# Fewer changes between full-width and column-tiled products in a two-layer attention kernel

## The chip, the cores and the metric

The kernel runs on one core of a Trainium2 chip. The metric is device time in microseconds for one execution over the whole input. Before the change the median of three runs is 2829.34 us (2828.06 to 2830.42), and the profiled execution spans 2826.2 us.

## The reference

The input `x` has 8 images of 256 channels and 96 x 96 points. Two residual layers follow each other, each behind a group norm `gn` (32 groups, no scale or shift). All arithmetic is in float32.

```
# layer 0
z   = gn(x)
q,k,v = fft2(w1 z + b1), fft2(w2 z + b2), fft2(w3 z + b3)      # 256 channels each
q,k = q/|q|, k/|k|                                             # norm over the 9216 points
a   = einsum('bhcn,bhdn->bhcd', q, k) * temperature            # 8 heads of 32 channels, no conjugate
a   = softmax(real(a)) + 1j * softmax(imag(a))
x   = x + w_out abs(ifft2(a v))
# layer 1
z   = gn(x)
q,k = softplus(Wq z + bq), softplus(Wk z + bk)                 # 32 channels each
v   = Wv z + bv                                                # 256 channels
x   = x + q (k v^T) / (q . (sum(k) + 1e-6))                    # linear attention
```

## The kernel before

The program handles one image after another (b = 0 to 7). Two large SBUF tiles, the arenas, hold an image each: the one being worked on, and in turn the rotated image `y` or the next `x`.

**No Fourier transform is carried out.** By Parseval's rule the logits and the norms of layer 0 follow from two 256 x 256 matrices: the Gram matrix of x with itself (for the norms) and the one of x with x read backwards in both directions (for the logits). `pair_sums(b)` forms the sum and the difference of each point with its mirror point (`eo`, on DVE or GpSimd, L305/L306), transposes them on TensorE (`eoT`, L338), evacuates them on ScalarE (L341) and adds their products into two PSUM accumulators (`products`, L319). Their sum and their difference are the two matrices, `cov[0]` and `cov[1]`. Both are symmetric, so only the blocks 00, 01 and 11 of 128 x 128 are accumulated.

**`attention(b)`** (L358) makes the small matrices of layer 0. It gets mean and deviation by group (`group_norm`, L258); lays the channel means on one partition (`mu`, L368); forms the constant terms of q and k (`qkm`, L379/L384); subtracts 2 HW mu mu^T from the accumulator by a product of one row (L395), which centres the sums; closes the accumulation with the last `products` (L397); forms `cov` (L403 to L406); transposes block 01 of both matrices to get block 10 (`covT`, L410); scales the rows by the deviation (L413); multiplies with the weights (`cw`, L424, for the norms, from four blocks; L435 for the logits); and then the softmax. The result is `mz`, which takes y to the channels of the attention output.

**`rotate(b)`** (L525) writes `y`, each row of the image times a constant matrix of its own, in steps of two rows: four transposes (`xr`, L547), evacuation on ScalarE (L558), four products with those matrices, `tm` (L550) and evacuation on DVE (L554). The `tm` tiles hold TR = 4 rows, in a pool of four buffers (L531), loaded through ScalarE's queue. The rows 0 to 3, 48 to 51 and 92 to 95 come last.

**`images(b)`** (L580) goes through 24 chunks of 384 points. `z` (L619) applies `mz` to `y`: real and imaginary parts of 16 channels of each head as full-width products (two of 128 columns), and channel 16 of the eight heads as one of 32 columns. For this `z16`, four chunks are computed at once on the four 32-column tiles of TensorE, every fourth chunk (L638 to L648); the tile `v16` has two buffers. Then come the modulus (ScalarE L660/L662/L663 and GpSimd L661), the output projection `po` (L631), the residual addition (L633) and the statistics for layer 1.

**`layer1(b)`** (L674) scales its weights by the deviation (`wkq` L683; `wvs` L724, from a resident copy `wv`), forms k and q on column tiles (`kq`, L711), and then goes through 18 steps of 128 points in four strands. A step transposes x (`xT`, L770, 8 transposes into two PSUM tiles), evacuates one tile on DVE (L775) and one on ScalarE (L773), and adds k x of the step before into `kx` (L748: four products on the four column tiles, each in two passes). k itself is transposed in six pieces (`kT`, L761), and softplus is finished along the way on DVE and ScalarE (L737 to L741). The loop around L748 is

```
if pend is not None:
    add_kx(*pend)
pend = (i, xt, kq(0, s)[...])
```

**`output(b)`** (L821) multiplies q by the reciprocal denominators (select on TensorE L826, product on DVE L828), forms `o` (L841), adds it to x on DVE and, through ScalarE, on GpSimd (L846 to L850), and stores.

**Order of the work.** `weave` advances one generator by what the other yields: the steps of `rotate(b)` fill `attention(b)`, and the steps of `pair_sums(b + 1)` fill the end of `images`, `layer1` and `output`. The last image has no following sums. A planner orders the instructions of each engine from priorities; where `manual_schedule` is named (PE in `attention`, and PE, DVE, GpSimd and SyncE in `output`) the order is that of the program. PSUM has five `ps` tiles and three `acc` tiles.

Of the kernel before, what the change touches and what calls it, by code (L numbers as in the profile page):

```python
# [47 lines left out]
F32 = mybir.dt.float32  # L49
AF = mybir.ActivationFunctionType  # L50
ALU = mybir.AluOpType
# [3 lines left out]
KC = 2  # L55
# [3 lines left out]
TR = 4  # L59
# [8 lines left out]
def two_layer_kernel(ctx: ExitStack, tc: tile.TileContext, x, w1t, b1, w2t, b2, w3, b3, wot, temp,  # L68
# [11 lines left out]
    assert C == KC * P and H == W and TW == 2 * CH and NT == 2 * NS and NC == 2 * NT and W <= P and PR == TR  # L80
# [4 lines left out]
    four = ctx.enter_context(tc.tile_pool(name="four", bufs=4))  # L85
# [39 lines left out]
    def ps_tile(name):  # L125
        return psum.tile([P, 512], F32, tag="ps", name=name)
# [60 lines left out]
    nc.vector.memset(half[0:W], 0.5 ** 0.5)  # L187
    epsb = const.tile([P, 1], F32, name="epsb")
# [4 lines left out]
    wv = const.tile([P, KC, C], F32, name="wv")  # L193
    nc.scalar.dma_start(out=wv, in_=wvt.rearrange("(k p) o -> p k o", p=P))
# [163 lines left out]
    def attention(b):  # L358
# [5 lines left out]
        w12, w3n = wl[:, :, 0:2 * C], wl[:, :, 2 * C:3 * C]  # L364
        nmean, rstd, mv, dm = yield from group_norm(st0, f"a{b}")
        pm = ps_tile(f"mu_{b}")
        for k in range(KC):
            nc.tensor.matmul(pm[0:1, k * P:(k + 1) * P], lhsT=mv[:, k, 0:1], rhs=ident, start=True, stop=True)  # L368
        scr = [ring_tile(f"scr{i}_{b}") for i in range(3)]
        mu = scr[0][0:1, 4 * C:6 * C].rearrange("p (c n) -> p c n", c=2)  # L370
        nc.vector.tensor_copy(mu[:, 0, :], pm[0:1, 0:C])
        nc.vector.tensor_scalar_mul(mu[:, 1, :], mu[:, 0, :], -2.0 * HW)
        nc.vector.tensor_mul(dm, dm, rstd)
# [3 lines left out]
        for k in range(KC):  # L377
            for m in range(KC):
                nc.tensor.matmul(pb[32 * m:32 * m + 1, 0:2 * P], lhsT=dm[:, k:k + 1],  # L379
                                 rhs=w12[:, k, :].rearrange("p (c n) -> p c n", c=2)[:, :, m * P:(m + 1) * P],  # L380
                                 start=(k == 0), stop=False, skip_group_check=True)
# [6 lines left out]
        qkm = [scr[1][32 * m:32 * m + 1, 0:6 * P].rearrange("p (i c n) -> p i c n", i=3, c=2) for m in range(KC)]  # L388
        for m in range(KC):
            nc.scalar.copy(qkm[m][:, 0], pb[32 * m:32 * m + 1, 0:2 * P].rearrange("p (c n) -> p c n", c=2))  # L390
            nc.vector.tensor_scalar_mul(qkm[m][:, 1], qkm[m][:, 0], 2.0 * HW)
            nc.vector.tensor_mul(qkm[m][:, 2], qkm[m][:, 0], qkm[m][:, 1])

        for m in range(KC):
            nc.tensor.matmul(acc[0][:, m * C:m * C + (KC - m) * P], lhsT=mu[:, 1, m * P:(m + 1) * P],  # L395
                             rhs=mu[:, 0, m * P:C], start=False, stop=False, skip_group_check=True)
        products(*pending, False, True)  # L397
        yield 1


        CW = 3 * P
        odd = scr[2][:, 4 * C:4 * C + CW]
        nc.scalar.copy(odd, acc[1][:, 0:CW])  # L403
        cov = scr[2][:, 0:4 * C].rearrange("p (c n) -> p c n", c=2)
        nc.vector.tensor_add(cov[:, 0, 0:CW], acc[0][:, 0:CW], odd)
        nc.vector.tensor_sub(cov[:, 1, 0:CW], acc[0][:, 0:CW], odd)  # L406
        yield 2
        pt = ps_tile(f"covT_{b}")
        for c in range(2):
            nc.tensor.transpose(pt[:, c * P:(c + 1) * P], cov[:, c, P:2 * P], ident)  # L410
        nc.scalar.copy(cov[:, :, CW:CW + P], pt[:, 0:2 * P].rearrange("p (c n) -> p c n", c=2))
        for k in range(KC):
            nc.vector.tensor_scalar_mul(cov[:, :, k * C:(k + 1) * C], cov[:, :, k * C:(k + 1) * C], rstd[:, k:k + 1])  # L413
# [7 lines left out]
        for m in range(KC):  # L421
            pv = ps_tile(f"cw_{b}_{m}")
            for k in range(KC):
                nc.tensor.matmul(pv, lhsT=block(0, k, m), rhs=w12[:, k, :], start=(k == 0), stop=(k == KC - 1))  # L424
# [3 lines left out]
            r = slice(32 * m, 32 * m + 1)  # L428
# [96 lines left out]
    def rotate(b):  # L525
# [4 lines left out]
        def load_r(h):  # L530
            tm = four.tile([W, TR, W + 1], F32, tag="tm", name=f"tm_{b}_{h}")  # L531
# [29 lines left out]
        last = (0, H // 2, H - TR)  # L561
        groups = [*(g for g in range(0, H, TR) if g not in last), *last]
        tms = [load_r(g) for g in groups[0:2]]
        pending = []
        for h in [g + i for g in groups for i in range(0, TR, 2)]:
            if h % TR == 0:
                i = groups.index(h)
                tm = tms.pop(0)
                if i + 2 < len(groups):
                    tms.append(load_r(groups[i + 2]))  # L570
# [9 lines left out]
    def images(b):  # L580
# [56 lines left out]
        for i in range(NC):  # L637
            if i % 4 == 0:  # L638
                p16 = ps_tile(f"z16_{b}_{i}")
                for k in range(KC):  # L640
                    for j, r in enumerate(blocks(2)):
                        apply(p16[r], k, 2, j, i + j)
                v16 = two.tile([P, CH], F32, tag="v16", name=f"v16_{b}_{i}")
                v3 = v16.rearrange("p (q h) -> p q h", h=H)
                nc.vector.tensor_add(v3, p16[:, 0:CH].rearrange("p (q h) -> p q h", h=H),
                                     tab16.unsqueeze(1).to_broadcast([P, PR, H]))
                nc.scalar.activation(v16, v16, AF.Square)
                nc.gpsimd.tensor_add(v3, v3, sg[2].unsqueeze(1).to_broadcast([P, PR, H]))  # L648
# [12 lines left out]
            nc.gpsimd.tensor_add(e[:, 0:2, :], e[:, 0:2, :], e[:, 2:4, :])  # L661
            nc.scalar.activation(e[:, 0:2, :], e[:, 0:2, :], AF.Sqrt)  # L662
            nc.scalar.activation(e[0:NH, 1, :], v16[32 * (i % 4):32 * (i % 4) + NH, :], AF.Sqrt)  # L663
            pending.append((i, e))
            if len(pending) > 2:
                project(*pending.pop(0))
# [7 lines left out]
    def layer1(b):  # L674
# [47 lines left out]
        for k in range(KC):  # L722
            nc.vector.tensor_scalar_mul(nmb[:, k, :], ones, nmean[:, k:k + 1])
            nc.vector.tensor_scalar_mul(wvs[:, k, :], wv[:, k, :], rstd[:, k:k + 1])  # L724
# [26 lines left out]
        pend = None  # L751
        softplus(0, 0)
        for s in range(NS):
# [9 lines left out]
            for i in range(s * CH // P, (s + 1) * CH // P):  # L763
                xt = [xt_slot(), xt_slot()]
# [17 lines left out]
        add_kx(*pend)  # L782
# [38 lines left out]
    def output(b, x, kq, rec, am):  # L821

        def normalize(s):
            t, g = divmod(s, 4)
            pd = ps_tile(f"rec_{b}_{s}")
            nc.tensor.matmul(pd[:, 0:CH], lhsT=sel8[32 * g:32 * g + 32, t * P:(t + 1) * P], rhs=rec[32 * g:32 * g + 32],  # L826
                             start=True, stop=True)
            nc.vector.tensor_mul(kq(1, s), kq(1, s), pd[:, 0:CH])  # L828

        for s in range(4):  # L830
            normalize(s)
        yield 1
        for s in range(4, NS):
            normalize(s)
        for s in range(NS):
            for m in range(KC):
# [6 lines left out]
                for j in range(NB):  # L843
# [91 lines left out]
```

## Time and profile before

| | |
|---|---|
| median of three runs | 2829.34 us |
| profiled span | 2826.2 us |
| TensorE (PE) busy | 2776.0 us |
| VectorE (DVE) busy | 2001.3 us |
| ScalarE (ACT) busy | 1358.4 us |
| GpSimd (POOL) busy | 871.0 us |
| one image, from one images stage to the next | 347.8 us |
| kx (L748) | 1152 records, 96.5 us |
| z and z16 (L619) | 2400 records, 600.9 us |
| cw for the norms (L424) | 64 records, 30.5 us |
| mu (L368), the one-row product (L395) | 4.8 us and 7.3 us |

A float32 product appears as two records (two passes), a transpose as one. A record such as `128*32 128x257` names the stationary tile (128 rows, 32 columns) and the moving tile. The busy time of PE counts the union of pipelined records, so that what one group costs is read better from the distance between its start and the next one's. "Idle before, releaser" is the time for which an engine waited, and for whom.

### The profile page before, as it was taken

How to read it: one execution, taken by the hardware profiler on the slowest of the kernel's cores; microseconds unless marked ns; L12 is line 12 of the kernel's file. 1: busy time of each engine (PE TensorE's matmuls, PEld its weight loads, DVE VectorE, ACT ScalarE, POOL GpSimd, SP SyncE). 2: the span in 40 equal slices, each digit the busy share in tenths (PEclk: the TensorE clock that was granted, in tenths of full speed). 3: DMA queues.
4: the chain of work that ended last, by engine and by line, in shares of the span. 5: the costliest groups of instructions: out<-in, count | busy, mean ns of one | idle time of the engine just before them, and what ended most of it. 6: DMA issues, size and time to landing. Idle time of an engine off the chain costs nothing.

```text
span 2826.2 us, 48343 instructions
## 1 busy us (share of the span) xinstructions
PE 2776.0 (98%) x18548; PEld 1984.4 (70%) x18548; DVE 2001.3 (71%) x4103; ACT 1358.4 (48%) x2066; POOL 871.0 (31%) x976
## 2 busy tenths in 40 slices
PE   8999999999999999999999999999999999999988
PEld 8965679656795667956688566785668856688556
DVE  7587765877658776587675876758766687666767
ACT  3455534555345553455533545345554455434553
POOL 4033430343303424035140351413514135231311
PEclk9999999999999999999999999999999999999997
DMA  5120151201412015120152201521015210151003
GB/s 168 37 72 11 33 183 42 72 5 48 168 47 72 3 46 172 47 68 2 46 175 51 62 3 46 177 59 52 3 46 179 63 45 3 57 171 28 1 3 135
DMA packets 196933, 190.72 MB, mean 67 GB/s; under 512 B 90272, under 2 KB 196704, under 8 KB 196704
## 3 DMA queue, kind: packets, MB, share of 16 engines
q1 hardware_dynamic: 128288, 162.25, 18.0%
q10 hardware_dynamic: 68416, 25.38, 3.8%
q8 instruction: 148, 2.42, 0.4%
q14 instruction: 81, 0.66, 0.1%
HBM read 112.01 MB, written 75.57 MB: 66 GB/s over the span
## 4 chain that ended last, share of the span: by engine, by line
PE 94%; DVE 2%; ACT 2%; issue 1%; DMA 0%; POOL 0%; POOLq 0%; ACTq 0%
PE z L619 20%; PE po L631 17%; PE acc L319 13%; PE y L550 11%; PE xr L547 6%; PE eoT L338 5%; PE kq L711 5%; PE xT L770 3%; PE o L841 3%; PE kx L748 3%; PE cw L424 1%; DVE arena L741 1%; ACT spu L739 1%; PE mz L511 1%; PE kT L761 1%
## 5 line engine op out<-in xcount | busy, mean ns | idle before, releaser
L619 PE MATMUL z<-arena,mz 128*128 128x384 f32 (+4 forms) x2400 | 600.9, 478 | 0.0
L631 PE MATMUL po<-e,wo 128*128 128x384 f32 x1536 | 529.8, 487 | 0.2 <-ACT e L662 0.2
L661 POOL TENSOR_TENSOR e<-e 128x768 f32<-128x768 f32 x192 | 348.4, 1816 | 511.6 <-ACT e L660 511.6
L619 PEld LDWEIGHTS z<-arena,mz 128*128 128x128 f32 (+1 forms) x2400 | 321.0, 163 | 254.1 <-issue 61.9
L550 PE MATMUL y<-tm,xT 96*128 96x97 f32 x3072 | 477.5, 261 | 1.7 <-POOL tm L533 1.5
L550 PEld LDWEIGHTS y<-tm,xT 96*128 96x128 f32 x3072 | 463.3, 192 | 13.1 <-issue 8.4
L319 PE MATMUL acc<-xT 128*128 128x256 f32 (+2 forms) x2368 | 442.8, 328 | 0.0
L656 DVE TENSOR_TENSOR e<-z,xT 128x768 f32<-128x768 f32 x384 | 366.2, 954 | 101.7 <-PE z L619 98.9
L631 PEld LDWEIGHTS po<-e,wo 128*128 128x128 f32 x1536 | 289.9, 190 | 197.3 <-DVE arena L633 1.2
L253 DVE BATCH_NORM_STATS2 st<-arena 128x6 f32<-128x384 f32 x768 | 406.4, 553 | 14.2 <-DMA arena<-in_x_dram 2.6
L547 PE MATMUL xr<-ident,arena 128*96 128x128 f32 x1536 | 414.2, 276 | 0.0
L319 PEld LDWEIGHTS acc<-xT 128*128 128x128 f32 (+1 forms) x2368 | 381.3, 191 | 36.1 <-issue 2.9
L558 ACT COPY xT<-xr 96x512 f32<-96x512 f32 x384 | 221.8, 582 | 303.7 <-PE xr L547 288.5
L554 DVE COPY arena<-y 128x384 f32<-128x384 f32 x384 | 213.6, 556 | 203.4 <-PE y L550 201.5
L305 POOL TENSOR_TENSOR eo<-arena 128x760 f32<-128x760 f32 x150 | 273.4, 1823 | 256.6 <-issue 133.5
L660 ACT ACTIVATE e<-e 128x1536 f32<-128x1536 f32 x192 | 284.6, 1482 | 101.2 <-DVE e L656 100.8
L662 ACT ACTIVATE e<-e 128x768 f32<-128x768 f32 x192 | 161.9, 843 | 334.3 <-POOL e L661 333.5
L633 DVE TENSOR_TENSOR arena<-arena,po 128x384 f32<-128x384 f32 x384 | 211.6, 553 | 95.7 <-PE po L631 71.9
L341 ACT ACTIVATE xT<-eoT 128x512 f32<-128x512 f32 x280 | 167.0, 597 | 194.9 <-PE eoT L338 192.9
L533 POOL COPY tm<-csn 96x4 f32<-96x4 f32 x192 | 38.1, 199 | 647.1 <-PE y L550 610.6
L547 PEld LDWEIGHTS xr<-ident,arena 128*96 128x96 f32 x1536 | 229.4, 150 | 10.9 <-issue 7.4
L850 POOL TENSOR_TENSOR arena<-arena,po 128x384 f32<-128x384 f32 x96 | 95.4, 1004 | 364.6 <-ACT po L849 364.6
(196 smaller groups left out, 3085.8 us busy)
## 6 DMA issues: line engine op xcount, KB each, us to landing
arena<-in_x_dram SPq DMA_DIRECT2D x184, 384.0 KB
out_dram<-arena SPq DMA_DIRECT2D x184, 384.0 KB
tm<-rt ACTq DMA_DIRECT2D x168, 144.0 KB
tm<-rt SPq DMA_DIRECT2D x24, 144.0 KB
arena<-in_x_dram SPq DMA_DIRECT2D x8, 288.0 KB
out_dram<-arena SPq DMA_DIRECT2D x8, 288.0 KB
wl<-in_w1t_dram SPq DMA_DIRECT2D x8, 256.0 KB
wl<-in_w2t_dram SPq DMA_DIRECT2D x8, 256.0 KB
```

Source lines behind the costliest of these rows:

```text
L253: nc.vector.bn_stats(out=st[:, k, c, :], in_=x_of(b)[:, k, c * CH:(c + 1) * CH])
L305: op(d[:, :, lo:hi, 1:W], x_t[:, :, ra:ra + n, 1:W], x_t[:, :, back, W - 1:0:-1])
L319: mm = nc.tensor.matmul(acc[c][:, m * C:m * C + (KC - m) * P], lhsT=t[0:np_, c, m * P:(m + 1) * P], rhs=t[0:np_, c, m * P:C], start=(first ...
L547: nc.tensor.transpose(pt[0:W, r * C + k * P:r * C + (k + 1) * P], x_of(b)[:, k, o:o + W], ident)
L550: nc.tensor.matmul(pu[:, o:o + W + 1], lhsT=gt[0:W, r, k * P:(k + 1) * P], rhs=tm[:, g % TR + r, :], start=True, stop=True)
L554: nc.vector.tensor_copy(y[:, :, :, g:g + 2], src[:, :, W - 1::-1, :])
L558: nc.scalar.copy(xt[0:W, :, 0:C], pt[0:W, :].rearrange("p (r n) -> p r n", r=2))
L619: mm = nc.tensor.matmul(out[:, o:o + n * W], lhsT=columns(mz, k, c, j), rhs=y[:, k, h * W:(h + n) * W], start=(k == 0 and o == 0), stop=(k ...
L631: nc.tensor.matmul(po[:, 0:CH], lhsT=wo[:, k, m * P:(m + 1) * P], rhs=e[:, k, :], start=(k == 0), stop=(k == KC - 1))
L656: nc.vector.tensor_add(e[:, 2 * c:2 * c + 2, :].rearrange("p t (q h) -> p t q h", h=H), pz[:, 0:CH].rearrange("p (q h) -> p q h", h=H).uns ...
L660: nc.scalar.activation(e, e, AF.Square)
L661: nc.gpsimd.tensor_add(e[:, 0:2, :], e[:, 0:2, :], e[:, 2:4, :])
```

## The change

It has five parts.

1. **Column tiles in larger groups.** z16 is computed for eight chunks at once, every eighth chunk, into two PSUM tiles and two `v16` tiles. k x is added for two steps together, every second step. So that three steps of xT can be held, two more slots come from the pool of the `tm` tiles, which gets three buffers of TR = 6 rows in place of four of 4. The room comes from the resident `wv`: its copy is loaded anew for each image, straight into `wvs`. The rotation goes through its rows in natural order.
2. **Sums not centred.** `mu` and the one-row product go; the last `products` and the forming of `cov` move to the front of `attention`. The constant terms get a second row, from the mean itself, which takes the mean's part off again: products of two rows with the factors +2 HW and -2 HW.
3. **Norms from three blocks.** A quadratic form in a symmetric matrix needs block 01 once, doubled; block 10 and its transpose are formed for the logits only.
4. **Order of the selects in `output`.** They come ahead of their multiplications.
5. **The last image's output.** It multiplies only the first piece of q at the front, and each further one between the units of `o`.

The diff, cut to its core:

```diff
-TR = 4
+TR = 6
...
-    four = ctx.enter_context(tc.tile_pool(name="four", bufs=4))
+    three = ctx.enter_context(tc.tile_pool(name="three", bufs=3))
...
-    wv = const.tile([P, KC, C], F32, name="wv")
-    nc.scalar.dma_start(out=wv, in_=wvt.rearrange("(k p) o -> p k o", p=P))
...
+        products(*pending, False, True)
         nmean, rstd, mv, dm = yield from group_norm(st0, f"a{b}")
-        pm = ps_tile(f"mu_{b}")
-        for k in range(KC):
-            nc.tensor.matmul(pm[0:1, k * P:(k + 1) * P], lhsT=mv[:, k, 0:1], rhs=ident, start=True, stop=True)
...
-        nc.vector.tensor_mul(dm, dm, rstd)
+        dmm = two.tile([P, KC, 2], F32, tag="dmm", name=f"dmm_{b}")
+        for c, v in enumerate((dm, mv[:, :, 0])):
+            nc.vector.tensor_mul(dmm[:, :, c], v, rstd)
+        CW = 3 * P
+        odd = scr[2][:, 4 * C:4 * C + CW]
+        nc.scalar.copy(odd, acc[1][:, 0:CW])
+        cov = scr[2][:, 0:4 * C].rearrange("p (c n) -> p c n", c=2)
+        nc.vector.tensor_add(cov[:, 0, 0:CW], acc[0][:, 0:CW], odd)
+        nc.vector.tensor_sub(cov[:, 1, 0:CW], acc[0][:, 0:CW], odd)
...
-        for m in range(KC):
-            nc.tensor.matmul(acc[0][:, m * C:m * C + (KC - m) * P], lhsT=mu[:, 1, m * P:(m + 1) * P],
-                             rhs=mu[:, 0, m * P:C], start=False, stop=False, skip_group_check=True)
-        products(*pending, False, True)
-        yield 1
...
-        for c in range(2):
-            nc.tensor.transpose(pt[:, c * P:(c + 1) * P], cov[:, c, P:2 * P], ident)
+        nc.tensor.transpose(pt[:, 0:P], cov[:, 1, P:2 * P], ident)
...
-            for k in range(KC):
-                nc.tensor.matmul(pv, lhsT=block(0, k, m), rhs=w12[:, k, :], start=(k == 0), stop=(k == KC - 1))
+            for k in range(m + 1):
+                nc.tensor.matmul(pv, lhsT=block(0, k, m), rhs=w12[:, k, :], start=(k == 0), stop=(k == m))
...
-        tms = [load_r(g) for g in groups[0:2]]
+        tms = [load_r(g) for g in range(0, 3 * TR, TR)]
...
-            if i % 4 == 0:
-                p16 = ps_tile(f"z16_{b}_{i}")
...
+            if i % 8 == 0:
+                v16 = []
+                p16 = [ps_tile(f"z16_{b}_{i + t}") for t in (0, 4)]
+                for t in range(2):
+                    for k in range(KC):
+                        for j, r in enumerate(blocks(2)):
+                            apply(p16[t][r], k, 2, j, i + 4 * t + j)
...
+        nc.sync.dma_start(out=wvs, in_=wvt.rearrange("(k p) o -> p k o", p=P))
...
-                xt = [xt_slot(), xt_slot()]
+                xt = [slots[2 * (i % 3) + jj] for jj in range(2)]
...
-                if pend is not None:
-                    add_kx(*pend)
-                pend = (i, xt, kq(0, s)[:, i % (CH // P) * P:(i % (CH // P) + 1) * P])
+                if len(pend) == 2:
+                    for p in pend:
+                        add_kx(*p)
+                    pend = []
+                pend.append((i, xt, kq(0, s)[:, i % (CH // P) * P:(i % (CH // P) + 1) * P]))
...
-        for s in range(4):
-            normalize(s)
-        yield 1
-        for s in range(4, NS):
-            normalize(s)
+        alone = b + 1 == B
+        if alone:
+            pds = [select(s, (acc_tile if s else ps_tile)(f"rec_{b}_{s}")) for s in range(4)]
+            normalize(0, pds[0])
...
+                if alone and m == 0 and s + 1 < NS:
+                    if s + 1 >= 4:
+                        pds.append(select(s + 1, acc_tile(f"rec_{b}_{s + 1}")))
+                    normalize(s + 1, pds[s + 1])
```

More of the change, by code (lines that the diff above doesn't have):

```diff
@@ L79, in two_layer_kernel @@
     NS = NC // NB
-    assert C == KC * P and H == W and TW == 2 * CH and NT == 2 * NS and NC == 2 * NT and W <= P and PR == TR
+    assert C == KC * P and H == W and TW == 2 * CH and NT == 2 * NS and NC == 2 * NT and W <= P and H % TR == 0
     const = ctx.enter_context(tc.tile_pool(name="const", bufs=1))
@@ L187, in two_layer_kernel @@
     nc.vector.memset(half[0:W], 0.5 ** 0.5)
+    hw2 = const.tile([P, 1], F32, name="hw2")
+    nc.vector.memset(hw2, -2.0 * HW)
+    for m in range(KC):
+        nc.vector.memset(hw2[32 * m:32 * m + 1], 2.0 * HW)
     epsb = const.tile([P, 1], F32, name="epsb")
@@ L364, in attention @@
         w12, w3n = wl[:, :, 0:2 * C], wl[:, :, 2 * C:3 * C]
+        products(*pending, False, True)
         nmean, rstd, mv, dm = yield from group_norm(st0, f"a{b}")
-        pm = ps_tile(f"mu_{b}")
-        for k in range(KC):
-            nc.tensor.matmul(pm[0:1, k * P:(k + 1) * P], lhsT=mv[:, k, 0:1], rhs=ident, start=True, stop=True)
         scr = [ring_tile(f"scr{i}_{b}") for i in range(3)]
-        mu = scr[0][0:1, 4 * C:6 * C].rearrange("p (c n) -> p c n", c=2)
-        nc.vector.tensor_copy(mu[:, 0, :], pm[0:1, 0:C])
-        nc.vector.tensor_scalar_mul(mu[:, 1, :], mu[:, 0, :], -2.0 * HW)
-        nc.vector.tensor_mul(dm, dm, rstd)
+        dmm = two.tile([P, KC, 2], F32, tag="dmm", name=f"dmm_{b}")
[7 more added lines that the diff above has]
+        nc.vector.tensor_sub(cov[:, 1, 0:CW], acc[0][:, 0:CW], odd)
         yield 2
@@ L378, in attention @@
             for m in range(KC):
-                nc.tensor.matmul(pb[32 * m:32 * m + 1, 0:2 * P], lhsT=dm[:, k:k + 1],
+                nc.tensor.matmul(pb[32 * m:32 * m + 2, 0:2 * P], lhsT=dmm[:, k, :],
                                  rhs=w12[:, k, :].rearrange("p (c n) -> p c n", c=2)[:, :, m * P:(m + 1) * P],
@@ L386, in attention @@
         yield 1
-        qkm = [scr[1][32 * m:32 * m + 1, 0:6 * P].rearrange("p (i c n) -> p i c n", i=3, c=2) for m in range(KC)]
+        qkm = [scr[1][32 * m:32 * m + 2, 0:6 * P].rearrange("p (i c n) -> p i c n", i=3, c=2) for m in range(KC)]
         for m in range(KC):
-            nc.scalar.copy(qkm[m][:, 0], pb[32 * m:32 * m + 1, 0:2 * P].rearrange("p (c n) -> p c n", c=2))
-            nc.vector.tensor_scalar_mul(qkm[m][:, 1], qkm[m][:, 0], 2.0 * HW)
+            nc.scalar.copy(qkm[m][:, 0], pb[32 * m:32 * m + 2, 0:2 * P].rearrange("p (c n) -> p c n", c=2))
+            nc.vector.tensor_scalar_mul(qkm[m][:, 1], qkm[m][:, 0], hw2[32 * m:32 * m + 2])
@@ L392, in attention @@
             nc.vector.tensor_mul(qkm[m][:, 2], qkm[m][:, 0], qkm[m][:, 1])
-        for m in range(KC):
-            nc.tensor.matmul(acc[0][:, m * C:m * C + (KC - m) * P], lhsT=mu[:, 1, m * P:(m + 1) * P],
-                             rhs=mu[:, 0, m * P:C], start=False, stop=False, skip_group_check=True)
-        products(*pending, False, True)
-        yield 1
[L401 to L404, printed above, removed]
@@ L405, in attention @@
-        nc.vector.tensor_add(cov[:, 0, 0:CW], acc[0][:, 0:CW], odd)
-        nc.vector.tensor_sub(cov[:, 1, 0:CW], acc[0][:, 0:CW], odd)
-        yield 2
-        pt = ps_tile(f"covT_{b}")
-        for c in range(2):
-            nc.tensor.transpose(pt[:, c * P:(c + 1) * P], cov[:, c, P:2 * P], ident)
-        nc.scalar.copy(cov[:, :, CW:CW + P], pt[:, 0:2 * P].rearrange("p (c n) -> p c n", c=2))
+        pt = ps_tile(f"covT_{b}")
+        nc.tensor.transpose(pt[:, 0:P], cov[:, 1, P:2 * P], ident)
@@ L412, in attention @@
+        nc.scalar.copy(cov[:, 1, CW:CW + P], pt[:, 0:P])
+        nc.vector.tensor_scalar_mul(cov[:, 0, 0:P], cov[:, 0, 0:P], rstd[:, 0:1])
+        nc.vector.tensor_scalar(cov[:, 0, P:2 * P], cov[:, 0, P:2 * P], scalar1=rstd[:, 0:1], scalar2=2.0,
+                                op0=ALU.mult, op1=ALU.mult)
+        nc.vector.tensor_scalar_mul(cov[:, 0, 2 * P:CW], cov[:, 0, 2 * P:CW], rstd[:, 1:2])
         for k in range(KC):
-            nc.vector.tensor_scalar_mul(cov[:, :, k * C:(k + 1) * C], cov[:, :, k * C:(k + 1) * C], rstd[:, k:k + 1])
+            nc.vector.tensor_scalar_mul(cov[:, 1, k * C:(k + 1) * C], cov[:, 1, k * C:(k + 1) * C], rstd[:, k:k + 1])
@@ L422, in attention @@
             pv = ps_tile(f"cw_{b}_{m}")
-            for k in range(KC):
-                nc.tensor.matmul(pv, lhsT=block(0, k, m), rhs=w12[:, k, :], start=(k == 0), stop=(k == KC - 1))
+            for k in range(m + 1):
+                nc.tensor.matmul(pv, lhsT=block(0, k, m), rhs=w12[:, k, :], start=(k == 0), stop=(k == m))
             nc.vector.scalar_tensor_tensor(prod[:, m, :], in0=pv, scalar=rstd[:, m:m + 1], in1=w12[:, m, :],
                                            op0=ALU.mult, op1=ALU.mult)
-            r = slice(32 * m, 32 * m + 1)
+            r = slice(32 * m, 32 * m + 2)
             part = prod[r, 0, :].rearrange("p (c n) -> p c n", c=2)[:, :, m * P:(m + 1) * P]
@@ L530, in load_r @@
         def load_r(h):
-            tm = four.tile([W, TR, W + 1], F32, tag="tm", name=f"tm_{b}_{h}")
+            tm = three.tile([P, TR * (W + 1)], F32, tag="tm", name=f"tm_{b}_{h}")[0:W].rearrange("p (r w) -> p r w", r=TR)
             (nc.scalar if b else nc.sync).dma_start(out=tm[:, :, 0:W], in_=window(h))
@@ L559, in step @@
                 return xt
-        last = (0, H // 2, H - TR)
-        groups = [*(g for g in range(0, H, TR) if g not in last), *last]
-        tms = [load_r(g) for g in groups[0:2]]
+        tms = [load_r(g) for g in range(0, 3 * TR, TR)]
         pending = []
-        for h in [g + i for g in groups for i in range(0, TR, 2)]:
+        for h in range(0, H, 2):
             if h % TR == 0:
-                i = groups.index(h)
                 tm = tms.pop(0)
-                if i + 2 < len(groups):
-                    tms.append(load_r(groups[i + 2]))
+            if h % TR == 4 and 3 * TR <= h - 4 + 2 * TR < H:
+                tms.append(load_r(h - 4 + 2 * TR))
             xt = step(h, pending.pop(0) if len(pending) == 2 else None)
@@ L637, in images @@
         for i in range(NC):
-            if i % 4 == 0:
-                p16 = ps_tile(f"z16_{b}_{i}")
[L640 to L648, printed above, removed]
+            if i % 8 == 0:
[5 more added lines that the diff above has]
+                            apply(p16[t][r], k, 2, j, i + 4 * t + j)
+                for t in range(2):
+                    v = two.tile([P, CH], F32, tag="v16", name=f"v16_{b}_{i + 4 * t}")
+                    v3 = v.rearrange("p (q h) -> p q h", h=H)
+                    nc.vector.tensor_add(v3, p16[t][:, 0:CH].rearrange("p (q h) -> p q h", h=H),
+                                         tab16.unsqueeze(1).to_broadcast([P, PR, H]))
+                    nc.scalar.activation(v, v, AF.Square)
+                    nc.gpsimd.tensor_add(v3, v3, sg[2].unsqueeze(1).to_broadcast([P, PR, H]))
+                    v16.append(v)
             if b + 1 < B and i % 2 and 3 <= i <= NT + 1:
@@ L662, in images @@
             nc.scalar.activation(e[:, 0:2, :], e[:, 0:2, :], AF.Sqrt)
-            nc.scalar.activation(e[0:NH, 1, :], v16[32 * (i % 4):32 * (i % 4) + NH, :], AF.Sqrt)
+            nc.scalar.activation(e[0:NH, 1, :], v16[i % 8 // 4][32 * (i % 4):32 * (i % 4) + NH, :], AF.Sqrt)
             pending.append((i, e))
@@ L723, in layer1 @@
             nc.vector.tensor_scalar_mul(nmb[:, k, :], ones, nmean[:, k:k + 1])
-            nc.vector.tensor_scalar_mul(wvs[:, k, :], wv[:, k, :], rstd[:, k:k + 1])
+            nc.vector.tensor_scalar_mul(wvs[:, k, :], wvs[:, k, :], rstd[:, k:k + 1])
         pv = ps_tile(f"bvs_{b}")
@@ L749, in add_kx @@
                                  rhs=xt[j // 2][:, j % 2, 0:C + 1], start=(i == 0), stop=(i == NS * CH // P - 1))
-        pend = None
+        extra = [three.tile([P, TR * (W + 1)], F32, tag="tm", name=f"xt{i}_{b}")[:, 0:2 * (C + 2)].rearrange(
+            "p (j n) -> p j n", j=2) for i in range(2)]
+        for t in extra:
+            nc.gpsimd.memset(t[:, :, C:C + 2], 1.0)
+        slots = [*(xT[:, i] for i in range(4)), *extra]
+        pend = []
         softplus(0, 0)
@@ L775, in layer1 @@
                         nc.vector.tensor_copy(xt[jj][:, :, 0:C], src)
-                if pend is not None:
-                    add_kx(*pend)
-                pend = (i, xt, kq(0, s)[:, i % (CH // P) * P:(i % (CH // P) + 1) * P])
+                if len(pend) == 2:
+                    for p in pend:
+                        add_kx(*p)
+                    pend = []
+                pend.append((i, xt, kq(0, s)[:, i % (CH // P) * P:(i % (CH // P) + 1) * P]))
                 yield 0.25
@@ L781, in layer1 @@
                 load_x(b + 1, NT // 2 - 1 - (s - NS // 2))
-        add_kx(*pend)
+        for p in pend:
+            add_kx(*p)
         if b + 1 < B:
@@ L821, in output, with select, normalize @@
     def output(b, x, kq, rec, am):
-        def normalize(s):
+        def select(s, pd):
             t, g = divmod(s, 4)
-            pd = ps_tile(f"rec_{b}_{s}")
             nc.tensor.matmul(pd[:, 0:CH], lhsT=sel8[32 * g:32 * g + 32, t * P:(t + 1) * P], rhs=rec[32 * g:32 * g + 32],
                              start=True, stop=True)
+            return pd
+        def normalize(s, pd):
             nc.vector.tensor_mul(kq(1, s), kq(1, s), pd[:, 0:CH])
-        for s in range(4):
-            normalize(s)
-        yield 1
-        for s in range(4, NS):
-            normalize(s)
+        alone = b + 1 == B
+        if alone:
+            pds = [select(s, (acc_tile if s else ps_tile)(f"rec_{b}_{s}")) for s in range(4)]
+            normalize(0, pds[0])
+        else:
+            for ss in (range(4), range(4, NS)):
+                pds = [select(s, ps_tile(f"rec_{b}_{s}")) for s in ss]
+                for s, pd in zip(ss, pds):
+                    normalize(s, pd)
+                if ss[0] == 0:
+                    yield 1
         for s in range(NS):
```

## The prediction

> **What bounds the kernel now.** I read the page's busy times and chain first.
>
> ```profile
> PE 2776.0 (98%) x18548; PEld 1984.4 (70%) x18548; DVE 2001.3 (71%) x4103; ACT 1358.4 (48%) x2066; POOL 871.0 (31%) x976
> ...
> PE 94%; DVE 2%; ACT 2%; issue 1%; DMA 0%; POOL 0%; POOLq 0%; ACTq 0%
> ```
>
> TensorE (PE) is the bound: 98% busy, 94% of the chain. So a microsecond off its instruction stream is a microsecond off the kernel, unless another engine holds PE at that place. Two questions follow: how much stream time goes, and where PE would then have to wait. For the first I read PE's timeline (start, length, instructions; the distance from one start to the next is the cost, because lengths overlap). Images stage, where z16 is folded into every fourth z:
>
> ```profile
> 2650.31 2.74 PE L631 MATMUL po<-e,wo 128*128 128x384 f32 x8
> 2652.99 4.28 PE L619 MATMUL z<-arena,mz 128*32 128x384 f32 x24
> 2657.10 2.75 PE L631 MATMUL po<-e,wo 128*128 128x384 f32 x8
> ```
>
> Eight full-width records take 2.58 us elsewhere in this view (0.3225 each). z16 is 16 records on four 32-column tiles side by side, so 4 x 0.3225 = 1.29 us of array time. The group takes 4.11 us, less 2.58 for the z in it, less 1.29, leaves 0.24; the po ahead takes 2.68 in place of 2.58, another 0.10. **One visit to the column tiles costs 0.34 us** beyond its work. The same for k x (kx) in the last batch, where nothing is woven in:
>
> ```profile
> 2760.60 1.09 PE L770 MATMUL xT<-ident,arena 128*128 128x128 f32 x8
> 2761.62 0.64 PE L748 MATMUL kx<-xT,arena 128*32 128x257 f32 x8
> 2762.19 1.09 PE L770 MATMUL xT<-ident,arena 128*128 128x128 f32 x8
> ```
>
> One step is 1.59 us. Eight transposes are 0.86 (sixteen in a row take 1.89 from 2781.12 to 2783.01, eight 1.02), and kx is 2 passes x 257 columns x 0.84 ns (0.3225 / 384) = 0.43. The rest, **0.30 us, is one visit**. The attention stage:
>
> ```profile
> 426.46 0.31 PE L275 MATMUL gv_a<-dv_a,gavg_sb 128*128 128x2 f32 x2
> 426.70 0.60 PE L368 MATMUL mu<-ident,mv_a 128*1 128x128 f32 x4
> 427.23 0.31 PE L547 MATMUL xr<-ident,arena 128*96 128x128 f32 x1
> ...
> 432.31 0.36 PE L550 MATMUL y<-tm,xT 96*128 96x97 f32 x2
> 432.60 0.92 PE L395 MATMUL acc<-scr 1*128 1x256 f32 x4
> 433.45 1.57 PE L319 MATMUL acc<-xT 96*128 96x256 f32 x8
> 434.86 0.28 PE L547 MATMUL xr<-ident,arena 128*96 128x128 f32 x1
> ...
> 441.25 1.91 PE L424 MATMUL cw<-wl,scr 128*128 128x512 f32 x4
> 442.99 0.27 PE L547 MATMUL xr<-ident,arena 128*96 128x128 f32 x1
> ```
>
> For the second question I took busy time by stretches of 7 us through the first batch's kx stage (columns: length, then PE, PEld, DVE, ACT, POOL busy):
>
> ```profile
> 326.00:333.00 7.00, 6.71 (x56) 5.02 (x57) 6.81 (x16) 4.43 (x9) 0.00 (x0) 1.00 0.00 0
> 333.00:340.00 7.00, 7.00 (x65) 5.15 (x66) 6.91 (x16) 4.35 (x9) 0.00 (x0) 1.00 0.25 69
> 340.00:347.00 7.00, 6.36 (x62) 4.30 (x60) 6.90 (x9) 3.30 (x7) 4.67 (x4) 1.00 0.35 103
> 347.00:354.00 7.00, 6.78 (x62) 5.03 (x63) 6.88 (x16) 4.35 (x8) 0.00 (x0) 1.00 0.61 169
> ```
>
> For 28 us VectorE (DVE) is busy 27.5 us with softplus and the xT copies, and PE already waits 1.15 us. This is the one stage where the page's "PE 98%" misleads. From 354 to 368 us DVE is at 32% and PE at 100%.
>
> **What the Trainium skill says.** "TensorEngine Tiling (Array Packing)", Key Properties: changing the tiling mode, not merely the tile, drains TensorE. The trace agrees, with 0.30 and 0.34 us for a visit. "Perfetto Trace Analysis", Identifying the Most-Contended Engine: matmul busy share is a poor measure of distance from the limit, since matmuls are pipelined; here the drains lie unseen inside the 98%. "TensorE: Matmul & The Clock Gate", Part 3, The mechanism: matmuls start and end strictly in order, so a kx waiting for its copy holds back all behind it; L748 waits for DVE 13 times in this trace. "SBUF — State Buffer", Terms: VectorE and GpSimd take turns at a shared port pair and the loser blocks; an L740 of 0.55 us takes 2.16 us at 341.85, under a POOL operation of 1.93 us, so DVE cannot be packed much denser there.
>
> **Part by part.**
> *Attention, eight times.* mu goes: gv_a to xr takes 0.77, and 0.23 where no mu stands between (424.98 to 425.21): 0.54. The K=1 products L395 go and the last L319 moves behind its fellows: y to xr is 2.55 now; y's own 0.20 and a plain L319 group's 1.31 remain: 1.04. cw loses one of four products: 1.74 / 2 = 0.87. One of two transposes in covT (0.22 us): 0.11. Sum 2.56; x 8 = 20.5 us.
> New waits there: PE reaches qkm 0.54 us sooner, but rstd comes at its old time. Now the product dm x rstd ends at 429.53 and qkm starts at 429.83, slack 0.30, so PE waits 0.24 at most if DVE's order is no worse. The two cov additions (0.56 each, L405/L406) move ahead of that chain, and mu's two copies (0.41 and 0.28) leave it; two additions in the way would be 1.1. Behind a waiting qkm the whole rotation is queued. I take 0.2 a batch, 1.6 in all (ends 0 and 8). **Net 18.9.**
> *z16 for eight chunks.* Six visits a batch become three: 24 x 0.34 = **8.2 us**. The second v16 tile must wait for ACT's L663 of the chunk before, some 5.9 us after that chunk's z (2706.97 to 2712.85); between them PE has po (2.58) and the z16 pair (2.9), and DVE's next e needs a z that ends 1.3 later still. So about 0.4 us of DVE wait, hidden under PE; ends 4 and 8.2.
> *kx for two steps.* In the two builds' instruction order, 142 visits become 73: 69 x 0.30 = 20.7 us if PE were free. It is not. DVE's work up to the copy of step 11 (ends 353.9, begun 325.7) is the same list in both. Up to there PE would be done 2.6 us before that copy (1.15 of present waits + 6 visits x 0.30, less the 0.43 of one kx that comes later), so it waits. Gained: DVE's present gaps, at most 0.5 us, plus after step 11 three visits less one extra kx, 0.9 - 0.43: 0.5 to 1.0. Some more may come where a port clash moves; I take 0.95 a batch for seven, 6.7 us. The last batch has DVE 29.0 of 31.0 us busy: at most 2.0, I take 1.0. **Sum 7.7**; ends 3 and 20.7.
> *Last output.* Six DVE multiplications (2.88 us, L828) stand before the first addition; now one does, and five go between units, where DVE idles 3.7 us in all. Takes 1.2 to 1.6 off the front, gives back 5 x (0.48 - 0.33) = 0.75. **1.0** (ends 0 and 2.5).
> *At nothing:* TR = 6 loads the same rows of tm in 128 issues in place of 192, each still six steps of 1.24 us ahead of use; the wv load (256 KB) goes out at the end of images, with 14 us until L724; extra xT slots, memsets and the smaller norm scaling lie beside PE-bound rotation; the selects keep their order on PE.
> Sum: 18.9 + 8.2 + 7.7 + 1.0 = 35.8. 2829.3 - 35.8 = **2793.5 us**.
>
> **Rivals.**
> (A) DVE does not hold kx back, because the copies are moved ahead of softplus: 13.0 more, 2780.5. For it: softplus of channel q is not needed until the stage's end. Against: in the build's order the copies stand among the same softplus operations.
> (B) New waits eat a good part: 1.0 a batch at qkm (-6.4), half of z16's gain (-4.1), nothing but 3 from kx (-4.7), no gain at the tail (-1.0): 2809.7. For it: three more dependences on an in-order DVE. Against: each has slack as worked out.
> (C) Slower: each pair of kx waits for its younger copy. One copy (0.69) at each of 73 visits is 50 us against 28.1 gained elsewhere: 2829.3 - 28.1 + 50 = 2851. For it: sixteen transposes in a row fill four PSUM tiles for one DVE and one ACT to empty. Against: a full step of transposes stands between a copy's source and its kx, as before.
>
> **How the numbers follow.** Forecast 70%, A 12%, B 13%, C 5%. Within the forecast the unknown costs add or take some 8 us. The range 2779 to 2807 holds the forecast and A (82%) and stops short of B and C. Faster 0.95 (forecast, A, B), within 0.2% 0.01, slower 0.04.
>
> **What would show it.** Right: mu and the K=1 products gone and PE's busy time down about 45; PE waits for DVE in the kx stage up from about 2 to 3 or 4 us a batch, DVE still near 98% until its last softplus; z16 pairs at about 2.9 us. Wrong: no new PE wait at kx (then A), PE idle at qkm or the first y of a batch, or a z16 pair that costs two visits. The forecast fails most readily if DVE's order in the kx stage is better or worse than "the same list, packed as before".

## The result, and the profile after

The changed kernel takes 2786.23 us (median, 2785.02 to 2789.91) against 2828.79 (2827.4 to 2830.42): 42.6 us less, ratio 0.9851, interval 0.9839 to 0.9864. A second series on another occasion gave 2788.97, ratio 0.9860 (0.9845 to 0.9875). The ten runs of the two series fall into two groups by the granted clock of PE, averaged over the run: 2784.41 to 2786.97 us at 0.997 or 0.998 (five of the first series and one of the second), 2788.57 to 2790.45 at 0.992 or 0.993. The prediction had 2793.5.

The page's busy times and its chain, for the changed kernel:

```profile
PE 2725.0 (98%) x18460; PEld 1969.4 (71%) x18460; DVE 1986.8 (71%) x4122; ACT 1350.2 (49%) x2066; POOL 858.6 (31%) x928
...
PE 92%; DVE 4%; ACT 2%; issue 1%; POOL 0%; DMA 0%; POOLq 0%; DVEq 0%; ACTq 0%
```

TensorE (PE) is busy 51 us less and still 98% of a shorter span (in the second series' profile 2734.4 us, 42 less: there the clock fell in the last image as it did before the change, and in the first profile it fell less); VectorE's (DVE's) share of the chain rose from 2% to 4%, a sign that another engine now holds PE somewhere. The PE timeline shows the pieces. The norms in the attention of the second batch (a batch is one image), where before two groups held four products in eight passes:

```profile
432.22 1.05 PE L420 MATMUL cw<-wl,scr 128*128 128x512 f32 x2
...
434.34 1.91 PE L420 MATMUL cw<-wl,scr 128*128 128x512 f32 x4
```

Three products are left in six passes, and no mu and no single-row product stands in the stage. In the last batch's images stage a z16 visit now serves eight chunks:

```profile
2633.75 2.74 PE L624 MATMUL po<-e,wo 128*128 128x384 f32 x8
2636.42 5.58 PE L612 MATMUL z<-arena,mz 128*32 128x384 f32 x44
2641.83 2.74 PE L624 MATMUL po<-e,wo 128*128 128x384 f32 x8
```

The group takes 5.41 us, of which 2.58 are the z folded into it: 2.83, and 0.09 more on the po ahead of it. That is 2.92 for two z16 groups of 1.29, so one visit of 0.34, the same as before, for twice the work. In the kx stage two steps stand together:

```profile
339.05 1.97 PE L773 MATMUL xT<-ident,arena 128*128 128x128 f32 x16
340.95 1.07 PE L746 MATMUL kx<-xT,arena 128*32 128x257 f32 x16
341.95 0.55 PE L764 MATMUL kT<-ident,arena 128*128 128x128 f32 x3
```

Two steps take 2.90 us where two single ones took 3.18: a visit is worth 0.28.

By stages, from the first product of one to the first of the next (kx: to VectorE's copy of the finished sum), a full batch, in us. zs is the small product of `mz` at the head of `images`, den the one for the denominators of layer 1:

| stage | before | after | difference | on record |
|---|---|---|---|---|
| rotation and attention, xr to zs, with the last products of the sums | 78.98 | 76.54 | -2.44 | -2.36 |
| images, zs to kq | 146.97 | 145.94 | -1.03 | -1.02 |
| kx stage, kT to the end of kx | 41.55 | 39.57 | -1.98 | -0.95 |
| output and sums, den to xr, without those products | 54.02 | 54.02 | 0 | 0 |

(After: xr to zs reads 75.23, and 1.31 of last products that now run ahead of xr is added; two of the eight batches save 0.4 less.) Every stage of a full batch but one is where the forecast put it. The kx stage gained twice its forecast, and two ends of the kernel moved: the first xr product came at 75.6 us before and at 78.4 after (78.1 to 79.3 in the nine profiles that have this start), of which only 1.3 is the moved products; the last output is shorter.

### The profile page after: what moved, and what is told of

Read it like the earlier page. It is cut to its first block, busy times and chain, and to the rows that moved or that the text cites. A ratio compares the mean times of both kernels' runs of the same rounds, so it can differ in the third digit from the quotient of the medians.

```text
span 2783.2 us, 47916 instructions
## 1 busy us (share of the span) xinstructions
PE 2725.0 (98%) x18460; PEld 1969.4 (71%) x18460; DVE 1986.8 (71%) x4122; ACT 1350.2 (49%) x2066; POOL 858.6 (31%) x928
## 4 chain that ended last, share of the span: by engine, by line
PE 92%; DVE 4%; ACT 2%; issue 1%; POOL 0%; DMA 0%; POOLq 0%; DVEq 0%; ACTq 0%
PE z L612 20%; PE po L624 18%; PE acc L322 13%; PE y L546 10%; PE xr L543 6%; PE eoT L341 5%; PE kq L709 5%; PE xT L773 4%; PE o L855 3%; PE kx L746 2%; DVE arena L739 1%; PE cw L420 1%; DVE arena L550 1%; PE kT L764 1%; PE mz L507 1%
## 5 line engine op out<-in xcount | busy, mean ns | idle before, releaser
L612 PE MATMUL z<-arena,mz 128*128 128x384 f32 (+2 forms) x2400 | 595.0, 476 | 0.0
L612 PEld LDWEIGHTS z<-arena,mz 128*128 128x128 f32 (+1 forms) x2400 | 325.7, 163 | 241.4 <-issue 42.4
L529 POOL COPY tm<-csn 96x6 f32<-96x6 f32 x128 | 24.2, 192 | 726.7 <-PE y L546 548.7
L341 PE MATMUL eoT<-ident,eo 128*128 128x128 f32 (+1 forms) x1184 | 186.8, 280 | 8.2 <-DVE eo L308 5.3
```

What stands on the lines that cost most here:

```text
L341: nc.tensor.transpose(pt[0:np_, c * C + k * P:c * C + (k + 1) * P], eo[:, c, k, i:i + np_], ident)
L612: mm = nc.tensor.matmul(out[:, o:o + n * W], lhsT=columns(mz, k, c, j), rhs=y[:, k, h * W:(h + n) * W], start=(k == 0 and o == 0), stop=(k ...
```

## Experiments

**What the pairs of kx bring alone, and what VectorE has to do with it.** Four kernels beside one another. The first is the changed kernel again.

> The changed kernel as it is, beside the three kernels that are read against it on the same chip. Every theory: 2786 us, 42 to 43 us less than before.

Measured: 2788.97 us, ratio 0.9860. This is what the next three are read against.

One step of kx at a time:

```diff
-                if len(pend) == 2:
+                if len(pend) == 1:
                     for p in pend:
```

> The changed kernel with k x for one step at a time again; the extra places for the copies stay. It gives the kx stage's share of the gain by itself. The prediction on record: +7.7 us on the changed kernel (VectorE holds the stage up to the twelfth copy, only the visits after it count). Second theory, from the two traces: kT to the end of the last kx fell by 2.0 us a batch and by 1.45 in the last, so +15.5 us. Third, VectorE holds nothing back: all 69 visits at 0.30, +20.7 us.

Measured: 2802.69 us, +13.7. The stage reads 40.8 to 41.6 us a batch in place of 39.5 to 39.7, 11.9 us more over the seven full batches. The term on record, 7.7, is refuted; the full price of all visits, 20.7, is not reached either; the second theory is nearest. VectorE's timeline, counted from kT's start, shows how. Its softplus list, with eleven xT copies in it, ends at 27.36 with single steps (26.6 to 26.8 in three batches where GpSimd's sums cost VectorE less) and at 26.50 with pairs. The operations are the same. With single steps VectorE stood 0.7 us in small gaps waiting for transposes, such as this one:

```profile
331.08 0.69 DVE L778 COPY xt<-xT 128x512 f32<-128x512 f32 x1 [0.19 <-PE xT L773]
```

With pairs there is no such gap (another of 0.2, ahead of the list's last operation, is in both). Under GpSimd it lost 2.79 and 2.62 us. From the list's end to the end of kx it is 14.2 with single steps and 13.05 with pairs. So 0.86 of the gain lies before that end and 1.13 after it.

The same two kernels without the rounding correction of the softplus, which leaves out part of the computation:

```diff
             nc.vector.tensor_scalar_add(u, e, 1.0)
-            nc.vector.scalar_tensor_tensor(e, in0=u, scalar=1.0, in1=e, op0=ALU.subtract, op1=ALU.subtract)
             nc.scalar.activation(u, u, AF.Ln, bias=zero)
-            nc.vector.tensor_sub(z, z, e)
             nc.vector.tensor_add(z, z, u)
```

> The changed kernel without the rounding correction of the softplus (z - ((u - 1) - e) is left out, two of its four VectorE operations): 24 operations of 0.47 us, 11.3 us of VectorE a batch, gone from the kx stage. If VectorE still holds this stage in the changed kernel, what TensorE waits there for VectorE goes: 8.3 us at the kT products, 5.2 at the xT transposes, 3.4 at kx, 16.9 in all, so 2770 us, up to 5 us less of it if ScalarE's logarithm takes VectorE's place. If VectorE no longer holds it: 2786, no change.

Measured: 2781.80 us, 7.2 less than the changed kernel, not 16.9. The list ends at 16.64 us, but the list of PE's waits over the whole kernel now begins with this (waiting line, releasing line, total us, times, longest):

```profile
PE xT L771 <- ACT arena L763: 8.4, 7, 1.2
```

It is new: transposes wait 1.2 us a batch for ScalarE's (ACT's) copy of kT. The timelines of the first batch show why. GpSimd (POOL) runs the even and odd sums of the next batch from 335.95 to 340.42; under it two VectorE additions of ones stretch from 0.62 to 2.25 us; ScalarE's logarithm waits 1.61 and 1.27 for them, and the kT copy stands behind the logarithm in ScalarE's order. By these lines shorter work on VectorE did not remove the hold because the hold is GpSimd's stretch, passed on from engine to engine; the last run below tests it.

> The same without the correction, and with k x for one step at a time. With VectorE out of the way each of the 69 visits should cost its full 0.30 us: 20.7 us more than the same kernel with pairs, where with VectorE's whole list it is 15.5 (from the traces) or 7.7 (on record). If the visits cost the same with and without VectorE's load, VectorE never hid any of them.

Measured: 2793.25 us, 11.5 more than with pairs; 20.7 fell. The stage is 40.04 us against 38.91, but the two differ in more than visits: with single steps VectorE loses 0.73 us under GpSimd, with pairs 2.66, and PE waits 0.4 and 1.4 a batch. This pair of runs does not give the price of a visit.

**The other parts alone.** Channel 16 for four chunks:

```diff
-            if i % 8 == 0:
+            if i % 4 == 0:
...
-                p16 = [ps_tile(f"z16_{b}_{i + t}") for t in (0, 4)]
+                p16 = [ps_tile(f"z16_{b}_{i}")]
```

> The changed kernel with channel 16 for four chunks at a time again. The prediction on record: 24 visits at 0.34 us come back, +8.2 us on the changed kernel (2786 to 2789 us); the traces gave 1.03 us a batch, +8.2 to 8.6. Rival: TensorE's time there was waiting anyway and the visits cost it nothing, 0.

Measured: 2796.17 us, ratio 0.9883 (0.9870 to 0.9897), 7 to 10 us more than the changed kernel's two medians. The stage reads 146.94 us in place of 145.94: 1.0 a batch, as on record; the rival is out.

Norms from four blocks:

```diff
-            for k in range(m + 1):
-                nc.tensor.matmul(pv, lhsT=block(0, k, m), rhs=w12[:, k, :], start=(k == 0), stop=(k == m))
+            for k in range(KC):
+                nc.tensor.matmul(pv, lhsT=block(0, k, m), rhs=w12[:, k, :], start=(k == 0), stop=(k == KC - 1))
```

(with both blocks transposed and scaled as before, none doubled; for each image one product, of two passes, and one transpose come back)

> The changed kernel with the norms from all four blocks again (sums still not centred): two more 128-row products of 512 columns and one more transpose... per batch one of the two products (0.87 us) and one transpose (0.11). The prediction on record: 0.98 a batch, +7.8 us. Rival: the scaling on VectorE and the copy on ScalarE, not the products, set the pace of this stretch; then under +4.

Measured: 2796.41 us, ratio 0.9880 (0.9865 to 0.9895). Rotation and attention read 76.21 in place of 75.24: 0.97 a batch, as on record.

The attention's text of before, whole:

> The changed kernel with the attention's text of before, whole: sums centred by mu, norms from four blocks, last products of the sums after the norms. The prediction on record: 2.56 a batch less 0.2 for new waits, +18.9 us; the traces gave 2.44 a batch, 2.0 in the first and third, +19.2. Taken with the run of the four-block norms, the centring alone should be 11 to 12 us, 1.4 to 1.5 a batch (mu 0.54 and the single-row products 1.04 were the price on record, less the waits).

Measured: 2808.41 us, ratio 0.9928 (0.9915 to 0.9940), 19 to 22 more. xr to zs reads 79.19, and 1.31 us of last products are back in it: 79.19 - 75.24 - 1.31 = 2.64 a batch, 2.1 and 2.3 in the first and third. Less the norms' 0.97, the centring is 1.67; mu and the single-row products were priced at 1.58. No wait took their place: PE's waits in this stretch of the changed kernel are 0.8 us at zs (0.7 before) and 0.1 at each of two other products (0.5 at one of them in the third batch, and 0.5 at a y of the first), none at qkm. But with the attention's text of before the stretch takes 79.19 us, and before the change 78.98. So what else changed in it, the rotation's order and loads among it, costs 0.2 a batch (0.1 in the first), where the prediction had nothing; which piece costs it was not separated.

The last output as the other seven:

```diff
-        alone = b + 1 == B
+        alone = False
```

> The changed kernel with the last output as the other seven (all selections and normalisations ahead of the first o product). The prediction on record: +1.0 us, ends 0 and 2.5; the traces gave 1.5. Either is near what five rounds can tell, so the profile's stretch from the first selection to the end is to decide: 33.2 us in the changed kernel, 34.2 or 34.7 here.

Measured: 2789.43 us, ratio 0.9860, no difference that the times can tell. The profile's stretch from the first selection to the end is 34.51 us, before 34.75, and 33.21 in the changed kernel. That looked like the 1.5 expected, and was not. The last stretch by engine (length, then PE, PEld, DVE, ACT, POOL busy, then PE's granted clock), first in the changed kernel's first profile:

```profile
2750.00:2783.00 33.00, 20.56 (x108) 12.38 (x108) 19.92 (x43) 5.75 (x12) 12.01 (x12) 0.86 0.81 286
```

then in its second, from the second series:

```profile
2753.00:2787.00 34.00, 25.85 (x108) 20.51 (x108) 21.36 (x44) 5.74 (x12) 11.94 (x12) 0.52 0.78 278
```

The same program has a clock of 0.86 there once and of 0.52 the other time. Before and the kernel with the plain output have 0.53 and 0.52. At that clock the changed kernel's stretch is 34.11: the reordered last output is worth about 0.4 us, and the other 0.9 us of the first profile go with the clock. Of the other kernels here with the new order and that clock seven read 33.7 to 34.1, but the one with the attention of before reads 34.5, so the 0.4 is not certain.

**What still holds the kx stage.** If GpSimd's stretch is the hold, the sums that fall into it should cost less on VectorE itself. In the changed kernel VectorE's timeline reads there:

```profile
341.56 1.56 DVE L739 TENSOR_TENSOR arena<-arena,spu 128x384 f32<-128x384 f32 x1
343.04 0.56 DVE L736 SCALAR_TENSOR_TENSOR arena<-spu,arena 128x384 f32<-128x384 f32 x1
343.52 1.95 DVE L735 TENSOR_SCALAR spu<-arena 128x384 f32<-128x384 f32 x1
```

The same L739 takes 0.55 us elsewhere and L735 0.35: GpSimd's two sums, 2.28 us from 340.42 and 2.11 from 343.15, cost VectorE 2.6.

```diff
-                eng = nc.vector if u in (0, 1, NT) or b == 0 and u % 2 else nc.gpsimd
+                eng = nc.vector if u in (0, 1, NT) or (u == 5 if b else u % 2) else nc.gpsimd
```

> The changed kernel with the even and odd sums of one group of rows (u = 5, the group whose sums fall into the kx stage) on VectorE in place of GpSimd. In the changed kernel VectorE loses 2.6 to 2.8 us a batch there while GpSimd runs them; on VectorE they take two operations of 0.87. Theory, what VectorE loses[...] holds the stage: VectorE's list ends 0.7 to 0.9 us sooner a batch at least, up to 1.75 if the two sums come after the list, so 5 to 12 us less in seven batches. Rival, VectorE's list no longer matters in the changed kernel: no change, or 1 to 2 us more.

Measured: 2773.45 us, ratio 0.9806 (0.9793 to 0.9820), 13 to 16 less than the changed kernel and beyond the range expected. The stage is 37.57 us in each of the seven full batches. PE's waits in the first batch's kx stage, before, then in the changed kernel, then in this one:

```profile
PE kx L748 <- DVE xT L775: 0.9, 2, 0.5
PE kT L761 <- DVE arena L741: 0.7, 1, 0.7
PE kx L748 <- ACT spu L739: 0.3, 1, 0.3
```

```profile
PE xT L773 <- DVE xT L778: 0.7, 1, 0.7
PE kT L764 <- DVE arena L739: 0.7, 1, 0.7
PE kx L746 <- DVE xt L778: 0.4, 1, 0.4
```

```profile
PE kT L764 <- DVE arena L739: 0.7, 1, 0.7
```

All but the wait for the first kT is gone, which stands ahead of the stretch that is counted. PE runs the same instructions in this stage in all three kernels, before in another order. From the changed kernel to this one the stage is 2.0 us shorter, while the listed waits that went are 1.1: what a stage lost is read from its length, not from the list alone. VectorE did hold the stage in the changed kernel: not by its own list alone, but by the 2.6 us that GpSimd added to it. ("SBUF — State Buffer", Terms, in the Trainium skill, has the two engines take turns at a shared port pair, the loser blocked; the lines above show the size.)

**Where the start was lost.** VectorE's and then PE's first lines on the sums of the first batch, changed kernel:

```profile
8.57 3.41 DVE L308 TENSOR_TENSOR eo<-arena 128x760 f32<-128x760 f32 x2
```

```profile
9.67 0.88 PE L341 MATMUL eoT<-ident,eo 128*128 128x128 f32 x3 [5.31 <-DVE eo L308]
12.13 1.51 PE L341 MATMUL eoT<-ident,eo 128*128 128x128 f32 x6 [1.59 <-POOL eo L309]
```

Before, the two sums took 0.95 each from 8.15. Now three small memsets (hw2) and half and epsb stand in front, and GpSimd's first sum begins at 8.89 in place of 9.35, in time to block VectorE's second. The edit puts the constants behind the first sums:

```diff
-    finish(pair_sums(0))
+    first = pair_sums(0)
+    for _ in range(4):
+        next(first)
+    constants()
+    finish(first)
```

(constants() holds the gsel copies and the memsets of half and hw2)

> The changed kernel with VectorE's small constants (twelve copies, five memsets) put behind the first even and odd sums. In the changed kernel the first transpose starts at 9.67 us and the next waits 1.6 us for GpSimd, as VectorE's second sum met GpSimd's first[...] (3.41 us for two). If that is where the start lost 1.5 us on before, VectorE's two sums now run at 6.4 to 8.2 us, ahead of GpSimd's at 8.9, and the first xr product comes 3 to 4 us sooner (78.4 to 78.9 now). Rival, x arrives too late for it: the first xr stays within 0.5 us.

Measured: 2783.57 us, ratio 0.9842 (0.9828 to 0.9855), 3 to 5 less than the two medians. The first xr comes at 74.8 us. VectorE and PE there:

```profile
6.06 1.82 DVE L311 TENSOR_TENSOR eo<-arena 128x760 f32<-128x760 f32 x2 [0.44 <-DMA arena<-in_x_dram]
```

```profile
7.15 0.67 PE L344 MATMUL eoT<-ident,eo 128*128 128x128 f32 x2 [2.80 <-POOL eo L312]
```

x was there all along (the rival falls). Which of the two put the start back in the changed kernel was not separated; VectorE's first sum began 0.4 us later, which is all that the memsets can have cost directly, and the rest came where its second sum met GpSimd's.

**Both edits, and the version that is faster than either kernel.**

> Both edits together, all of the computation kept: the sum of the two, 2773 to 2780 us if both theories hold, as the two stages lie 250 us apart. Were they to share a cause the sum would not be reached.

Measured: 2768.97 us (2767.07 to 2770.11), ratio 0.9789 (0.9776 to 0.9803): 60 us less than before and 17 to 20 less than the changed kernel, the sum of the two edits as measured, and nothing of the computation is left out. It lies below the range expected, because the sums on VectorE alone had already brought more than theirs.

> The same without the rounding correction of the softplus (left out, as before). With pairs and without the correction, TensorE waited 1.2 us a batch for ScalarE's copy of kT, which stood behind a logarithm that waited for VectorE, which GpSimd held up. With these sums on VectorE that wait should go: kT to the end of kx 37.5 to 38.0 us a batch instead of 38.9, some 7 us less than without the two edits for that part, 2770 us in all. If ScalarE itself was the limit the wait stays and the stage keeps its 38.9.

Measured: 2765.61 us, ratio 0.9777 (0.9763 to 0.9790). The wait for ScalarE is gone with GpSimd's sums and the stage is 37.15 us, a little below the range expected: ScalarE was not the limit. Against 40.04 with single steps, less their 0.39 of waits, the nine visits saved are worth 2.5 us, 0.28 each (an estimate, since that kernel still had GpSimd's sums). The correction itself, half of VectorE's softplus operations, costs only 0.4 us a batch once GpSimd is out of the way.

## Why the prediction was right, and where it was not

**Right, by its own steps.** PE's stream sets the time, and most of what leaves it leaves the span: about 45 us less of busy time were expected, 42 came with a clock at the end like that of before (51 with the higher one). A visit costs 0.28 to 0.34 us beyond its work, read three ways (pairs side by side in the timeline, z16 undone, the stages without waits). z16: 8.2 on record, 1.0 a batch measured. Norms: 0.98 on record, 0.97 measured. Attention as a whole: 18.9 net on record, 18.7 from the traces. That it agrees so well is in part luck: undoing the text brings 20, the 0.2 us a batch of waits feared at qkm did not come, and about as much was lost to what else changed in that stretch, which stood at nothing. The rivals failed for the reasons given: no wait at qkm or z16 (B), and kx does not wait a copy per pair (C).

**Wrong: the size of the kx term**, 7.7 on record, 13.7 measured by undoing it. Two steps of its sum failed, one before the copy of step 11 and one after it. The first reads "DVE's work up to the copy of step 11 (ends 353.9, begun 325.7) is the same list in both" and "Gained: DVE's present gaps, at most 0.5 us". The list is indeed the same; its end is not fixed. Before, VectorE was full only by its busy time: records overlap the next by some 0.08 us (a softplus operation of 0.55 begins 0.47 after the one before it), which covers gaps in a sum of lengths. By starts there were 0.85 us of gaps, and in 0.67 of them VectorE waited for PE's transposes, while PE a little later waited for VectorE. Pairs free PE early in the stage, transposes come sooner, and these gaps are gone: with 0.17 from a smaller loss under GpSimd the list ends 0.86 us sooner a batch.

The second step is "after step 11 three visits less one extra kx, 0.9 - 0.43". No extra kx came. The copy of step 11 ends at 351.5 us in the changed kernel:

```profile
350.52 0.64 PE L746 MATMUL kx<-xT,arena 128*32 128x257 f32 x8
351.55 0.64 PE L746 MATMUL kx<-xt,arena 128*32 128x257 f32 x8 [0.39 <-DVE xt L778]
```

The pair's older half did not wait for that copy, and seven steps of kx follow it, as before. So this part gained 1.13 in place of 0.47, and the two together 2.0 a batch in place of 0.95.

In other words, nine visits saved are worth 2.5 us a batch by the stages without waits, and PE gave back only some 0.5 of it to VectorE, where the prediction let it give back 1.75 (9 x 0.30 less 0.95). So "PE waits for DVE in the kx stage up from about 2 to 3 or 4 us a batch" was wrong in size: the listed waits are the same, 1.15 before and 1.14 after, without the first kT's 0.7; by the lengths of the stages (41.54 against 39.65, which is 40.04 less 0.39, and 39.57 against 37.15) it is 1.9 before and 2.4 after. That VectorE holds the stage was right (rival A, all 69 visits free, is out), but what makes it hold is GpSimd's sums, 2.6 to 2.8 us a batch in both kernels; without them the stage is 2.0 us shorter still. One sum in this part is off by a little: 1.15 + 6 x 0.30 - 0.43 is 2.5 and not 2.6.

**Too large: the last output**, 1.0 on record, about 0.4 at an equal clock. The prediction's own working gives less than it took: 1.2 to 1.6 less 0.75 is 0.45 to 0.85.

**Left out: the start.** "At nothing: ... memsets" overlooked that VectorE's constants stand ahead of the first sums, with nothing on PE to hide them. By the first xr, less the moved products, that is some 1.5 us in the first profile and 2.0 in the second; the kernel with the attention of before, which moves no products, has it 2.0 later than before too. There is one profile of before, and the same start varies by about 1 us from profile to profile.

The sum of parts, 18.7 + 8.2 + 13.7 + 0.4 - 2.0 = 39, agrees with the second series, 2788.97 us, 38 to 40 less. The first series is some 3 us better, and that goes with the clock of the last image, which no part of the change was meant to move.

## What to carry to other kernels

An engine at 98% in a stage is not a fixed bound when it feeds on the engine that it bounds: measure its gaps from start to start, and ask which of them the change itself closes. When such an engine does hold a stage, look first for stretched records of its own under another engine's work: here, moving that work was worth as much as the whole pairing (14 us), and halving the softplus list without moving it half of that. Price what a change puts at the very start apart, where PE has nothing else to do. And compare the granted clock before a few microseconds are put down to a cause.

## What was not expected of the hardware

A VectorE operation of 0.35 us (L735, one tile) took 1.95 us and one of 0.55 us 2.16 us while GpSimd ran a 128x760 addition. In the two kernels without the correction, which differ there only in the order of kx, VectorE lost 2.66 us with pairs and 0.73 with single steps to the same two additions.

And the granted clock of the last 34 us was 0.51 to 0.53 in eleven of the fourteen profiles, 0.60 in one and 0.86 in two, for the same program 0.52 once and 0.86 once. From the first zs of the last image to the end those two profiles of one program took 235.6 and 231.4 us.
